# A graph network's dense output bank, its hot nodes' products and its counting one-hots, rearranged

## The chip, the cores and the metric

The kernel runs on one core of a Trainium2 chip. The metric is the device time of one execution in microseconds, the median over several runs. A profile comes from one more execution, recorded by the hardware profiler; its own time is given beside its span. Instructions run on TensorE (PE; its weight loads are PEld), VectorE (DVE), ScalarE (ACT), GpSimd (POOL) and SyncE (SP, which only issues DMAs). [...]

## The reference

There are 6250 nodes with 256 features, 100000 edges sorted by destination, and eight edge types. Three layers of a relational graph network run on x; the result is added to x and normalised. Then an attention layer and a second normalisation follow, which the change does not touch.

```python
for l in range(n_layers):                                   # 3
    xr = jnp.einsum('nd,rde->rne', x, W_rel[l])             # 8 matrices of 256 x 256
    msg = xr[edge_type, src]                                # one row per edge
    agg = jax.ops.segment_sum(msg, dst, num_segments=x.shape[0])
    x = jax.nn.relu(agg + x @ W_root[l] + bias[l])
```

The destinations are `6250 * u**2` for uniform `u`, sorted: low node numbers have very many edges. The first 4608 edges all end in about 16 nodes.

## The kernel before

**Order of operations.** The kernel sums source rows first and multiplies after: for each destination node and edge type it sums the source rows of x (the array S in SBUF, features on partitions), and a dense stage multiplies a node tile of 128 nodes by the eight relation matrices and the root matrix. Node tiles are called j, 49 of them; edges go in tiles t of 128, in groups of four.

**A step.** The loop of `layer` at L680 runs 193 steps in each of three layers, 188 of them with a group of edges. All instructions are written out by hand in this order (`manual_schedule`, L232), and each engine keeps it. A step does this:
- counting and hot products, if they are due (L681 to L684, below)
- `gather` (L474): four indirect DMAs on GpSimd bring the 4 x 128 source rows into a `msg` buffer, of which there are eight
- `onehot` (L458) on VectorE, for the group four steps later
- `finish` (L574) for a node tile whose dense products ended in the step before: bias on VectorE, relu on ScalarE, a store on SyncE; in the last layer also the sum with x and the normalisation. Then `clear` on ScalarE zeroes the tile's place in S
- `windows` (L483) on TensorE: rows times one-hot, into PSUM banks `pw`, of which there are four. A step uses one to four of them
- dense pieces (L704): up to six matmuls of the current tile, or more if several tiles are waiting; no further tile is begun in a step in which one ends
- `add` (L500) on VectorE: four additions of the windows into S. Each must wait for dense matmuls of a tile that is still being read from S, since the place in S is a register's value
- `turn` (L526): transposes of x rows for dense tiles that come up.

There are two interleaved streams of groups, each with its own ring in S (four and three node tiles long).

**The dense output.** `dense` (L553) takes a PSUM tile `pd` from the pool `ps_d`, which has one bank (L199). It issues two root products (L558) and sixteen relation products (L562). The bank is free again when `finish` has read it (L576, L579; L587 in the last layer).

**Hot nodes.** The edges of the first 36 edge tiles are not gathered. In layer 0, `count` (L609) makes a matrix A: how often each source node appears for each of the 16 hot nodes and each type. For a hot node n and each edge tile t that may hold edges of n, VectorE writes a one-hot `sel` of 392 columns (L622; three buffers) and, when t is new, a one-hot `low` (L618; 16 buffers); TensorE adds the product of both into a bank `ph` (L624); ScalarE copies the sum to A (L627). There are 138 pairs of n and t; steps from 56 on do two pairs each (COUNT_AT, L681), which ends at step 125. In every layer `products` (L630) multiplies A with all rows of x: 13 loads of four node tiles into a `msg` buffer through SyncE (L642, L640 for the partial last one), then the products (L651), all 49 into one bank `ph`. It moves on at every second step from 130 (HOT_AT, L683): the products of a load come two steps after the load, just before the next load. At the end ScalarE copies the sum (L653), TensorE transposes it (L657) and VectorE adds it to S (L660). The pool `ps_h` with one bank (L198) serves `count` and `products`.

**PSUM.** Eight banks: four `pw`, one `ph`, one `pd`, one for transposes (`pt`), one for a constant row (`iota`).

Of the kernel before, what the change touches and what calls it, by code (L numbers as in the profile page):

```python
# [10 lines left out]
F32 = mybir.dt.float32  # L11
I32 = mybir.dt.int32
BF16 = mybir.dt.bfloat16
AF = mybir.ActivationFunctionType
ALU = mybir.AluOpType
AX = mybir.AxisListType
PSUM = bass.MemoryType.PSUM
# [3 lines left out]
P = 128  # L21
# [3 lines left out]
PAD = 32  # L25
MARGIN = 800
HOT = 16
LOWS = 16
COUNT_AT = 56
HOT_AT = 130  # L30
NEAR = 450
# [123 lines left out]
def fast(tc, const, pl, x, xs, src, dst, edge_type, w_rel, w_root, bias, weight,  # L155
         attn_l, attn_r, out, flag):
    nc = tc.nc
    N, D = x.shape
    E = src.shape[0]
    L, R = w_rel.shape[0], w_rel.shape[1]  # L160
    H, DH = attn_l.shape
    KC = D // P
    NT, T, CH, WMAX = pl.NT, pl.T, pl.CH, pl.WMAX
    KR = KC * R

    with ExitStack() as top:
        tab = top.enter_context(tc.tile_pool(name="tab", bufs=1))
        ident = tab.tile([P, P], F32, name="ident")
        idx = tab.tile([P, CH * P], I32, name="idx")
        key = tab.tile([P, CH * P], F32, name="key")  # L170
        pos = tab.tile([1, CH * P], I32, name="pos")
        iota_p = tab.tile([P, 1], F32, name="iota_p")
        eps = tab.tile([P, 1], F32, name="eps")
        bias_b = tab.tile([P, L, D], F32, name="bias_b")
        w1x = tab.tile([P, KC, D + 2 * H], F32, name="w1x")
        altab = tab.tile([P, NT, H], F32, name="altab")

        psi = top.enter_context(tc.tile_pool(name="psi", bufs=1, space=PSUM))
        iota = psi.tile([P, max(R * WMAX, NT * R)], F32, name="iota")
        hk = tab.tile([P, pl.TH], F32, name="hk")  # L180
        hl = tab.tile([P, pl.TH], F32, name="hl")

        dram = top.enter_context(tc.tile_pool(name="lanes", bufs=1, space=DRAM))
        lane = dram.tile([NT * P], I32, name="lane")
        with tc.tile_pool(name="ps_p", bufs=2, space=PSUM) as ps_p:
            tables(tc, pl, ps_p, src, dst, edge_type, ident, idx, key, pos, iota, iota_p,
                   lane, hk, hl, flag, R, H)
        y = dram.tile([NT * P, D], F32, name="y")

        with ExitStack() as s:  # L190
            wp = s.enter_context(tc.tile_pool(name="wp", bufs=1))
            sp = s.enter_context(tc.tile_pool(name="sp", bufs=1))
            mp = s.enter_context(tc.tile_pool(name="mp", bufs=8))
            op = s.enter_context(tc.tile_pool(name="op", bufs=AHEAD + 2))
            xp = s.enter_context(tc.tile_pool(name="xp", bufs=3))
            hp = s.enter_context(tc.tile_pool(name="hp", bufs=1))
            ps_w = s.enter_context(tc.tile_pool(name="ps_w", bufs=4, space=PSUM))
            ps_h = s.enter_context(tc.tile_pool(name="ps_h", bufs=1, space=PSUM))  # L198
            ps_d = s.enter_context(tc.tile_pool(name="ps_d", bufs=1, space=PSUM))  # L199
            ps_t = s.enter_context(tc.tile_pool(name="ps_t", bufs=1, space=PSUM))  # L200


            S = [sp.tile([P, KR, n * P + PAD], F32, name=f"S{f}") for f, n in enumerate(NS)]

            hold = {j: sp.tile([P, KR, P], F32, name=f"hold{j}") for j in sorted(pl.shared(pl.TM))}


            A = hp.tile([P, NT, HOT * R], F32, name="A")

            nc.vector.memset(eps, EPS)  # L210
            for t in S:
                nc.scalar.memzero(t)
            nc.sync.dma_start(bias_b, bias.rearrange("l d -> (l d)").partition_broadcast(P))
            fold_weights(tc, mp, w1x, weight, attn_l, attn_r)

            def load_w(l):
                wr = wp.tile([P, KC, R, D], F32, name="wr")
                wo = wp.tile([P, KC, D], F32, name="wo")
                for k in range(KC):
                    nc.scalar.dma_start(  # L220
                        wr[:, k], w_rel[l, :, k * P:(k + 1) * P, :].rearrange("r p e -> p r e"))
                    nc.scalar.dma_start(wo[:, k], w_root[l, k * P:(k + 1) * P, :])
                return wr, wo

            groups = pl.order()

            ready = {}
            for i, (f, g) in enumerate(groups):
                for j in pl.reach(g):
                    ready[f, j] = i  # L230

            with tc.manual_schedule():  # L232
                for l in range(L):
                    wr, wo = load_w(l)
                    layer(tc, pl, l, l == L - 1, groups, ready, S, hold, A, hk, hl, idx, key, pos, iota, ident,
                          wr, wo, bias_b, x, xs, eps, w1x, altab, y,
                          mp, op, xp, hp, ps_w, ps_d, ps_t, ps_h, H)

        attention(tc, pl, lane, dst, idx, iota_p, ident, eps, w1x, altab, y, out, H)

# [199 lines left out]


def layer(tc, pl, l, final, groups, ready, S, hold, A, hk, hl, idx, key, pos, iota, ident, wr, wo,
          bias_b, x, xs, eps, w1x, altab, y, mp, op, xp, hp, ps_w, ps_d, ps_t, ps_h, H):
    nc = tc.nc
    N, D = x.shape
    KC = D // P
    R = wr.shape[2]
    NT = pl.NT
# [125 lines left out]
    def finish(j, pd):  # L574
        n = rows(j)
        nc.vector.tensor_tensor(pd[:, :D], pd[:, :D], bias_b[:, l], ALU.add)  # L576
        if not final:
            h = xp.tile([P, D], F32, name="h")
            nc.scalar.activation(h, pd[:, :D], AF.Relu)  # L579
            nc.sync.dma_start(xs[l + 1][j * P:j * P + n, :], h[:n])  # L580
            return
        xin = xp.tile([P, D], F32, name="xres")
        if n < P:
            nc.vector.memset(xin, 0.0)
        nc.sync.dma_start(xin[:n], x[j * P:j * P + n, :])
        z = xp.tile([P, D], F32, name="h")
        nc.vector.scalar_tensor_tensor(z, pd[:, :D], 0.0, xin, op0=ALU.max, op1=ALU.add)  # L587
        st = xp.tile([P, 6], F32, name="st")
        mv = xp.tile([P, 2], F32, name="mv")
        rs = xp.tile([P, 1], F32, name="rs")  # L590
        nc.vector.bn_stats(st, z)
        nc.vector.bn_aggr(mv, st)  # L592
        nc.scalar.activation(rs, mv[:, 1:2], AF.Sqrt, bias=eps)  # L593
        nc.vector.reciprocal(rs, rs)
        yt = xp.tile([P, D], F32, name="yt")
        nc.vector.tensor_scalar(yt, z, mv[:, 0:1], rs, op0=ALU.subtract, op1=ALU.mult)
        nc.sync.dma_start(y[j * P:(j + 1) * P, :], yt)
        return yt
# [9 lines left out]

    def count():  # L609

        lows = {}
        for n in range(HOT):
            tiles = pl.hot_tiles(n)
            pc = ps_h.tile([P, 512], F32, name="ph")
            for t in tiles:
                if t not in lows:
                    lows[t] = hp.tile([P, P], BF16, name="low", bufs=LOWS)
                    nc.vector.tensor_scalar(lows[t], iota[:, :P], hl[:, t:t + 1], None,  # L618
                                            op0=ALU.is_equal)
                    assert len([u for u in lows if u >= tiles[0]]) <= LOWS  # L620
                oh = hp.tile([P, NT * R], BF16, name="sel", bufs=3)
                nc.vector.tensor_scalar(oh, iota[:, :NT * R], float(512 * n), hk[:, t:t + 1],  # L622
                                        op0=ALU.add, op1=ALU.is_equal)
                nc.tensor.matmul(pc[:, :NT * R], lows[t], oh, start=(t == tiles[0]),  # L624
                                 stop=(t == tiles[-1]))
                yield
            nc.scalar.copy(A[:, :, n * R:(n + 1) * R],  # L627
                           pc[:, :NT * R].rearrange("p (j r) -> p j r", r=R))

    def products():  # L630

# [11 lines left out]
                    "(t p) d -> p t d", p=P))  # L643
            return t

        ph = ps_h.tile([P, 512], F32, name="ph")
        for js in loads:
            t = load(js)
            yield
            for n, j in enumerate(js):  # L650
                nc.tensor.matmul(ph[:, :D], A[:, j], t[:, n], start=(j == 0), stop=(j == NT - 1))  # L651
        sums = hp.tile([P, D], F32, name="sums")
        nc.scalar.copy(sums, ph[:, :D])  # L653
        yield
        pt = ps_t.tile([P, 4 * P], F32, name="pt")
        for k in range(KC):
            nc.tensor.transpose(pt[:, k * P:(k + 1) * P], sums[:, k * P:(k + 1) * P], ident)  # L657
# [22 lines left out]
    for i in range(NG + 5):  # L680
        for _ in range(2 if i >= COUNT_AT else 0):  # L681
            next(counting, None)
        if i >= HOT_AT and i % 2 == 0:  # L683
            next(hot, None)  # L684
        for j in sorted(fetch.get(i, []), reverse=True):
            held[j] = load_rows(j)
# [479 lines left out]
```

## Time and profile before

| | us |
|---|---|
| median of three runs | 3737.52 (3736.14 to 3748.91) |
| profiled execution | 3772.36 |
| its span | 3770.6 |
| TensorE busy | 2943.0 (78%) |
| TensorE weight loads | 2596.9 (69%) |
| GpSimd busy | 2155.9 (57%) |
| VectorE busy | 1740.8 (46%) |
| ScalarE busy | 481.0 (13%) |

The layers lie at about 60 to 1240, 1240 to 2405 and 2405 to 3600 us of the span, the attention behind them. Steps 56 to 126 of layer 0, with the counting, are 393.3 to 866.4 us; steps 130 to 158, with the hot products, follow in each layer.

A row of a group gives line, engine, operation, what is written and read, shape and number; then the busy time in us and the mean of one in ns; then the idle time of the engine just before these instructions and what ended most of it. In a timeline the columns are start and length in us, engine, line and operation, the number of instructions merged, and in brackets the idle time before and what ended it. "issue" stands where the profile names nothing that ended a wait, "remote" where it names no instruction. A matmul of f32 is recorded as two instructions. Ends of matmuls are modelled.

### The profile page before, as it was taken

The numbers are of one execution on the slowest core, as the hardware profiler recorded it, in microseconds if no ns is written. First come the engines' busy times: TensorE is split into PE (matmuls) and PEld (weight loads), VectorE is DVE, ScalarE is ACT, GpSimd is POOL, SyncE is SP. The second block draws the span as 40 slices with busy tenths as digits, with TensorE's granted clock in tenths as the row PEclk, the third lists the DMA queues.
The fourth block names the chain that finished last, engine by engine and source line by source line (L and its number), as shares of the span: only waits on it lengthen the run. The fifth ranks groups of instructions, "written<-read, shape, count | busy, mean of one in ns | idle before, by whom it ended". The sixth has DMA issues, their size and how long they took to land. (4 is left out here: it accounts for less than half of the span.)

```text
span 3770.6 us, 45208 instructions
## 1 busy us (share of the span) xinstructions
PE 2943.0 (78%) x15503; PEld 2596.9 (69%) x15504; DVE 1740.8 (46%) x4043; ACT 481.0 (13%) x646; POOL 2155.9 (57%) x2256
## 2 busy tenths in 40 slices
PE   3898878788777489888788866578988888877862
PEld 3787766677666378777677766567877777766752
DVE  5454555554333244444444323245555454433467
ACT  1111111110000011111111000011111110100033
POOL 5666555555664566666665666355666566566502
PEclk8999998889877699998988977789998898887786
DMA  4333222324432333333333433233333333443332
GB/s 124 103 105 101 87 87 88 90 85 123 134 96 73 106 100 105 101 104 102 100 97 115 138 103 99 86 90 102 104 110 101 101 108 98 124 128 103 89 121 94
DMA packets 201423, 389.11 MB, mean 103 GB/s; under 512 B 42661, under 2 KB 127652, under 8 KB 201188
## 3 DMA queue, kind: packets, MB, share of 16 engines
q0 software_dynamic: 107424, 293.48, 26.7%
q1 hardware_dynamic: 85832, 85.17, 7.1%
q10 hardware_dynamic: 7932, 7.48, 0.6%
q8 instruction: 129, 2.11, 0.2%
q14 instruction: 106, 0.87, 0.1%
HBM read 360.31 MB, written 25.65 MB: 102 GB/s over the span
## 5 line engine op out<-in xcount | busy, mean ns | idle before, releaser
L478 POOL DMA_INDIRECT msg<-x,idx x1492 | 1417.3, 950 | 954.7 <-issue 388.9
L495 PE MATMUL pw<-oh,msg 128*128 128x112 f32 (+6 forms) x8952 | 1461.7, 321 | 395.3 <-issue 188.5
L495 PEld LDWEIGHTS pw<-oh,msg 128*128 128x128 f32 x8952 | 1370.8, 213 | 504.8 <-issue 263.4
L507 DVE TENSOR_TENSOR S<-S,pw 128x224 f32 (+6 forms) x2238 | 954.3, 426 | 1598.6 <-remote 501.3
L562 PE MATMUL pd<-wr,S 128*128 128x256 f32 x4704 | 1180.9, 401 | 47.3 <-issue 31.5
L562 PEld LDWEIGHTS pd<-wr,S 128*128 128x128 f32 x4704 | 937.4, 203 | 198.9 <-issue 51.1
L478 POOL DMA_INDIRECT msg<-in_x_dram,idx x746 | 708.8, 950 | 487.1 <-issue 190.3
L462 DVE TENSOR_TENSOR oh<-iota,key 128x672 f32<-128x672 f32 (+8 forms) x564 | 388.6, 691 | 30.6 <-issue 16.9
L571 ACT ACTIVATE S<-S 128x2048 uint32<-128x2048 uint32 x150 | 285.0, 1900 | 0.1
L532 ACT COPY xT<-pt 128x256 f32<-128x256 f32 x196 | 72.8, 372 | 1254.5 <-PE pt L530 422.6
L558 PE MATMUL pd<-wo,xT 128*128 128x256 f32 x588 | 182.8, 439 | 45.7 <-ACT h L579 20.0
L579 ACT ACTIVATE h<-pd 128x256 f32<-128x256 f32 x98 | 37.7, 384 | 1172.3 <-DVE pd L576 753.7
L576 DVE TENSOR_TENSOR pd<-pd,bias_b 128x256 f32<-128x256 f32 x147 | 63.1, 429 | 219.6 <-PE pw L495 102.9
L558 PEld LDWEIGHTS pd<-wo,xT 128*128 128x128 f32 x588 | 116.4, 217 | 65.8 <-ACT h L579 24.8
L624 PE MATMUL ph<-sel,low 128*128 128x392 bf16 x138 | 43.3, 346 | 85.3 <-DVE sel L622 58.9
L847 POOL TENSOR_TENSOR pd<-yg,td 128x1792 f32<-128x1792 f32 x7 | 28.3, 4048 | 115.4 <-DVE td L845 48.9
L605 PE MATMUL pt<-w1x,xT 128*128 128x4 f32 x196 | 35.5, 287 | 66.4 <-ACT xT L532 44.3
L605 PEld LDWEIGHTS pt<-w1x,xT 128*128 128x128 f32 x196 | 31.2, 228 | 79.3 <-ACT xT L532 53.2
L622 DVE TENSOR_SCALAR sel<-iota,hk 128x392 bf16<-128x392 f32 x138 | 80.3, 613 | 0.0
L593 ACT ACTIVATE rs<-mv,eps 128x1 f32<-128x1 f32 x49 | 14.4, 295 | 482.5 <-DVE mv L592 338.9
L624 PEld LDWEIGHTS <-low 128*128 128x128 bf16 x138 | 13.2, 98 | 87.0 <-issue 48.5
L651 PE MATMUL ph<-msg,A 128*128 128x256 f32 x294 | 72.8, 391 | 0.0
(155 smaller groups left out, 749.7 us busy)
## 6 DMA issues: line engine op xcount, KB each, us to landing
msg<-x,idx POOLq DMA_INDIRECT x1492
x<-h SPq DMA_DIRECT2D x96, 128.0 KB
xin<-x SPq DMA_DIRECT2D x96, 128.0 KB
msg<-x SPq DMA_DIRECT2D x24, 512.0 KB
msg<-in_x_dram,idx POOLq DMA_INDIRECT x746
y<-yt SPq DMA_DIRECT2D x49, 128.0 KB
yg<-y SPq DMA_DIRECT2D x7, 896.0 KB
wr<-in_L_gnn_W_rel_dram ACTq DMA_DIRECT2D x6, 1024.0 KB
```

Of the source, the lines that this page charges most:

```text
L462: nc.vector.tensor_tensor(oh[:, :len(g), :w], iota[:, :w].unsqueeze(1).to_broadcast([P, len(g), w]), key[:, g[0]:g[-1] + 1].unsqueeze(2).t ...
L478: nc.gpsimd.indirect_dma_start(out=msg[:, q, :], out_offset=None, in_=table, in_offset=bass.IndirectOffsetOnAxis(ap=idx[:, t:t + 1], axis=0))
L495: nc.tensor.matmul(pw[:, k * w:(k + 1) * w], msg[:, q, k * P:(k + 1) * P], oh[:, q, :w], start=True, stop=True)
L507: ins = nc.vector.tensor_tensor(o, o, pw.rearrange("p (a b) -> p a b", b=W), ALU.add)
L532: nc.scalar.copy(xT.rearrange("p k n -> p (k n)"), pt[:, :D])
L558: nc.tensor.matmul(pd[:, :D], xT[:, k], wo[:, k], start=(k == 0), stop=False)
L562: i = nc.tensor.matmul(pd[:, :D], s[:, k * R + r], wr[:, k, r], start=False, stop=(k == KC - 1 and r == R - 1))
L571: i = nc.scalar.memzero(cols(f, j))
L576: nc.vector.tensor_tensor(pd[:, :D], pd[:, :D], bias_b[:, l], ALU.add)
L605: nc.tensor.matmul(pt[:, :H], yT[:, k], w1x[:, k, D + H:D + 2 * H], start=(k == 0), stop=(k == KC - 1))
L622: nc.vector.tensor_scalar(oh, iota[:, :NT * R], float(512 * n), hk[:, t:t + 1], op0=ALU.add, op1=ALU.is_equal)
L651: nc.tensor.matmul(ph[:, :D], A[:, j], t[:, n], start=(j == 0), stop=(j == NT - 1))
```

## The change

Three things change.

The pool `ps_h` goes, and `ps_d` has two banks. Dense tiles, the counts of a hot node and the hot products all take a bank from it, under the name `pd`.

In `count`, seven `sel` buffers (SELS) and eighteen `low` buffers (LOWS) let the one-hots of a pair be written five pairs (two and a half steps) before the pair's product. The bank is taken at a node's first product, and the copy to A stands right after its last.

In `products`, each load of four node tiles is summed in a bank of its own, and VectorE adds that bank to `sums` in SBUF (a copy for the first). The generator now moves on at every step: load at an even step, products at the odd step after it, addition at the next even step, before the next load. The final copy on ScalarE goes; the transposes follow the last addition in the same step.

Beside that the tiles `xres` and `yt` of the last layer have two buffers, not three.

```diff
-LOWS = 16
+SELS = 7
+LOWS = 18
...
-            ps_h = s.enter_context(tc.tile_pool(name="ps_h", bufs=1, space=PSUM))
-            ps_d = s.enter_context(tc.tile_pool(name="ps_d", bufs=1, space=PSUM))
+            ps_d = s.enter_context(tc.tile_pool(name="ps_d", bufs=2, space=PSUM))
...
-        xin = xp.tile([P, D], F32, name="xres")
+        xin = xp.tile([P, D], F32, name="xres", bufs=2)
...
-        yt = xp.tile([P, D], F32, name="yt")
+        yt = xp.tile([P, D], F32, name="yt", bufs=2)
...
-        lows = {}
-        for n in range(HOT):
-            tiles = pl.hot_tiles(n)
-            pc = ps_h.tile([P, 512], F32, name="ph")
-            for t in tiles:
+        lows, made, pc = {}, [], None
+        pairs = [(n, t) for n in range(HOT) for t in pl.hot_tiles(n)]
+        for m in range(len(pairs) + SELS - 2):
+            if m < len(pairs):
+                n, t = pairs[m]
                 if t not in lows:
                     lows[t] = hp.tile([P, P], BF16, name="low", bufs=LOWS)
                     nc.vector.tensor_scalar(lows[t], iota[:, :P], hl[:, t:t + 1], None,
                                             op0=ALU.is_equal)
...
-                oh = hp.tile([P, NT * R], BF16, name="sel", bufs=3)
+                oh = hp.tile([P, NT * R], BF16, name="sel", bufs=SELS)
                 nc.vector.tensor_scalar(oh, iota[:, :NT * R], float(512 * n), hk[:, t:t + 1],
                                         op0=ALU.add, op1=ALU.is_equal)
+                made.append((n, t, oh))
+
+            if m >= SELS - 2:
+                n, t, oh = made.pop(0)
+                tiles = pl.hot_tiles(n)
+                if t == tiles[0]:
+                    pc = ps_d.tile([P, 512], F32, name="pd")
                 nc.tensor.matmul(pc[:, :NT * R], lows[t], oh, start=(t == tiles[0]),
                                  stop=(t == tiles[-1]))
-                yield
-            nc.scalar.copy(A[:, :, n * R:(n + 1) * R],
-                           pc[:, :NT * R].rearrange("p (j r) -> p j r", r=R))
+                if t == tiles[-1]:
+                    nc.scalar.copy(A[:, :, n * R:(n + 1) * R],
+                                   pc[:, :NT * R].rearrange("p (j r) -> p j r", r=R))
+            yield
...
-        ph = ps_h.tile([P, 512], F32, name="ph")
+        sums = hp.tile([P, D], F32, name="sums")
         for js in loads:
             t = load(js)
             yield
+            ph = ps_d.tile([P, 512], F32, name="pd")
             for n, j in enumerate(js):
-                nc.tensor.matmul(ph[:, :D], A[:, j], t[:, n], start=(j == 0), stop=(j == NT - 1))
-        sums = hp.tile([P, D], F32, name="sums")
-        nc.scalar.copy(sums, ph[:, :D])
-        yield
+                nc.tensor.matmul(ph[:, :D], A[:, j], t[:, n], start=(n == 0), stop=(j == js[-1]))
+            yield
+            if js[0] == 0:
+                nc.vector.tensor_copy(sums, ph[:, :D])
+            else:
+                nc.vector.tensor_tensor(sums, sums, ph[:, :D], ALU.add)
...
-        if i >= HOT_AT and i % 2 == 0:
+        if i >= HOT_AT:
             next(hot, None)
```

## Prediction

> **What bounds the kernel now.** First the page: the profiled execution took 3772.4 us, its span 3770.6, 34.8 us over the median of the runs (3737.5); I take differences from it in us and subtract them from the median. TensorE is busy 2943.0 us (78%), GpSimd 57%, VectorE 46%. By stages, TensorE is 85 to 91% busy in 300 us early in each layer (100 to 400, 1400 to 1700, 2500 to 2800) and the clock's mean is 0.876. Next the timeline: the gather of a step is issued 35 to 50 us before the windows that use it, seven steps ahead, and its last packet lands 2.4 us after the issue. So the gathers wait for buffers that TensorE frees, and TensorE with the waits in its own queue sets the time. The chain of waits holds only the last 5 us and tells nothing here.
>
> Then the windows view over the same steps (56 to 126) of the three layers; columns are the stretch, its length, busy us of PE, PEld, DVE, ACT, POOL, granted clock, DMA share, GB/s:
>
> ```profile
> 393.30:866.40 473.10, 385.22 (x2001) 335.31 (x2001) 260.30 (x552) 55.20 (x72) 257.67 (x272) 0.89 0.29 86
> 1615.30:2026.10 410.80, 344.85 (x1865) 307.33 (x1866) 181.49 (x382) 47.98 (x57) 258.64 (x273) 0.92 0.34 100
> 2795.60:3222.30 426.70, 363.17 (x1985) 326.02 (x1986) 216.30 (x500) 53.62 (x77) 260.00 (x274) 0.90 0.35 102
> ```
>
> Only layer 0 counts, and takes 62.3 us more than layer 1 for it: 40.4 of TensorE work, 21.9 of idleness. The waits of TensorE there (total, times, longest):
>
> ```profile
> PE ph L624 <- DVE sel L622: 55.9, 48, 4.5
> PE ph L624 <- issue: 17.5, 15, 4.0
> PE ph L624 <- DVE low L618: 6.1, 2, 3.3
> ```
>
> They are nearly all of its 87.9 idle us. The timeline of one step shows why:
>
> ```profile
> 828.00 1.89 PE L562 MATMUL pd<-wr,S 128*128 128x256 f32 x8
> 829.51 0.10 PEld L624 LDWEIGHTS <-low 128*128 128x128 bf16 x1
> 829.93 2.12 DVE L507 TENSOR_TENSOR S<-S,pw 128x336 f32 x4 [3.37 <-PE pd L562]
> 831.97 1.15 DVE L622 TENSOR_SCALAR sel<-iota,hk 128x392 bf16<-128x392 f32 x2
> 832.64 0.33 PE L624 MATMUL ph<-sel,low 128*128 128x392 bf16 x1 [2.75 <-issue]
> 833.54 0.33 PE L624 MATMUL ph<-sel,low 128*128 128x392 bf16 x1 [0.57 <-ACT A L627]
> ```
>
> VectorE may add to S only after the dense matmuls have read it, the one-hots stand behind those adds, the count's matmul behind the one-hot, and all windows behind it. Last, what the first dense matmul of a tile waits for, in the whole kernel:
>
> ```profile
> L558 PE MATMUL pd<-wo,xT 128*128 128x256 f32 x588 | 182.8, 439 | 45.7 <-ACT h L579 20.0 <-issue 12.9 <-DVE h L587 12.6
> ```
>
> I worked out from the loop in which step each tile starts and is evacuated, and set the gaps at L558 beside it: every one of over 0.3 us but one (0.7 us, step 182 of layer 0) lies in a step in which a tile starts while the one before it is evacuated; there are 26 such steps a layer. There the tile's bank is free only when bias (VectorE) and relu (ScalarE) are through with it; in the last layer the reader is the sum with x, L587.
>
> [...] The trace has half and full speed only; fewer gaps may add speed, which I don't count. [...]
>
> **One-hots ahead (count).** Removed from TensorE's path: its gaps before L624, 71.0 us before the first product of a step and 14.3 before the second, 85.3. No instruction is removed: 138 one-hots (617 ns) and 36 lows (339 ns) stay, two and a half steps ahead of their products; LOWS grows since a low lives that much longer; the stage ends two steps later (127), before the hot loads at 130. Three things come back. First, relu waits: the count holds one of the two banks, so dense has one, as before. In ten steps a tile starts while the last is evacuated. After the dense end VectorE does adds 2.1, two one-hots 1.2, next step's one-hot 0.85, bias 0.43, then relu 0.38 and handovers: about 5.0 us. TensorE without the stall does products 0.4 and windows 2.4 and is there after some 3.2: 1.8 us in ten steps, 18. Second, the copy of a count (0.49 us plus handovers, 0.7) stands between two nodes in the same step, eight times if the same bank is taken: 5. Third, window banks: the first add frees one 0.5 us after the dense end; the products fill that time. Nothing; if they don't, 70 x 0.2 = 14. That would leave 62. But layer 1 counts nothing and still idles 65.9 us here, in stretches where adds wait for TensorE up to 11 us. Layer 1 plus products (69 pairs x 0.4, by 0.49 for a pair and 0.1 hidden, = 28) plus 18 - 6.8 = 11 more of relu waits (6.8 are in layer 1's time) is 449.8: gain 23. I take 33, nearer to the second, as those stretches may also come here. Bounds 12 and 65.
>
> **Second bank for dense.** Removed: the 45.7 us at L558 less what stays: 4.0 in layer 0's count stage, where the count holds the other bank, 0.2 in the hot stage, where a part holds it, and the 0.7 of step 182. That is 40.8: 9.9 in layer 0, 18.2 in layer 1, 12.6 in layer 2. Elsewhere the two banks alternate, and a tile is evacuated two or more steps before its bank returns. Bias and relu themselves stay (429 and 384 ns) but hide behind the new tile's first products. What comes next is the add after the dense part, which moves forward by the same amount, and with it the windows' banks; so nearly all counts: 34. Bounds 0 (rival 2) and 41.
>
> **Hot products in parts.** Added: 13 instructions a layer on VectorE, 39 x 424 ns (the row of L587, a read of the same width[...]) = 16.5 us; three ScalarE copies (373 ns) go. VectorE is 36 to 39% busy in the three hot stages; if nothing hid them, 16.5. A part is a bank's sum over four node tiles, added to sums in SBUF. Products use the loaded rows one step after the load, not two. Each load stays at its even step and its SyncE place behind the last stores. From issue to the next step's windows there are at least 9.3 us for the full loads, and a pair of loads lands 3 to 8 us after its first issue (about 4.5 to 7 for most): no wait, at worst 2 us in four. The last, partial load has 5.8, 5.2 and 3.6 us and lands after 4.8 to 5.9: 3 us in all. At the end the transposes now wait for the last part's add behind the step's adds, 2.5 us x 3 = 7.5; in return the old transposes' waits, 17.6 us, go in part: say 8. The rows' buffers come free a step sooner, worth nothing as gathers are three steps ahead there. Sum: a loss of 3; bounds a loss of 20 and a gain of 8. Deeper xres and yt buffers are given up at no cost: finishes two apart are five steps or more apart, a yt is read after two. If that cover failed, one VectorE wait of some 3 us for each of 49 tiles, 147.
>
> **Sum.** 33 + 34 - 3 = 64 us, 1.7%: 3772.4 becomes 3708, the median 3737.5 becomes 3673.5. A measurement of this kernel tells about 0.5% (18.7 us) from no change.
>
> **Rivals.** (1) The count's stall moves: what TensorE no longer waits for at L624 it waits for at windows and relu, gain 10 instead of 33: 3696.5. For it: layer 1's idleness. Against: in the step shown nothing else was late. (2) The pool gives the next tile the bank just freed, so the second bank does nothing: 3737.5 - (33 - 3) = 3707.5. Against: eight msg buffers are used in turn, seven steps deep. (3) More gain: 62 for the count, 41 for dense, 3 lost, and a little clock: 3635. For it: the idle sums; against: layer 1. (4) Slower: the hot loads come late. One step of lead is lost for each of 39 loads; if SyncE, behind stores that wait for relu (104.7 us of waits in layer 0's hot stage), issues them so late that each product waits 3 us, that is 117, and 3673.5 + 117 = 3790 follows. It makes the kernel slower by over 0.5% above (64 + 18.7)/39 = 2.1 us a load. Leads of 9 us against 7 of landing speak against it.
>
> **Chances.** Likeliest case (gain 40 to 85) 0.60; rival 1 0.14; rival 2 0.09; rival 3 0.09; rival 4 0.05; nothing gained for reasons not seen 0.03. Below 3718.8 lie the likeliest, rival 3 and most of 1 and 2: faster 0.84; same 0.10; slower 0.06. Range 3642 to 3714: the likeliest case alone is 3652 to 3697; the range goes on to rivals 1 and 2 and leaves out rivals 3 and 4 and what is unseen, 0.17.
>
> **What would show it.** Right: the gaps before the count's matmul (now from ph to pd) fall from 85 to under 15 us, that stage from 473 to about 440; L558 idle falls to about 10, what is left lying in steps 56 to 126. Wrong: L558 gaps unchanged; L651 with gaps at all (now 0.4 us in sum); new gaps at L495 after DVE adds; layers 1 and 2 not shorter by 10 to 18 us each. What would break the whole sum is layer 1's idleness: if it belongs to a busy TensorE, what is taken off one wait returns in another.

## The result, and the profile after

Over eight runs each, the kernel before takes 3738.38 us (3722.18 to 3759.57), the changed one 3696.16 us (3683.15 to 3716.37). The ratio is 0.9883, with a 95% interval of 0.9847 to 0.9919: 42 us faster, where 64 was forecast. The profiled execution of after took 3689.81 us, its span 3688.0, its granted clock 0.877 (0.876 before). It was 6 us below the median of its kernel; that of before, 3772.36, was 34 above its own and above all eight of its runs. So the two spans differ by 82.6 us and the medians by 42: about 40 us of what the pair of profiles shows is the spread between executions, and a stage's difference from it can carry any part of that.

First the page of after, part 1: busy us, share of the span and instructions of each engine.

```profile
PE 2921.8 (79%) x15503; PEld 2587.1 (70%) x15504; DVE 1746.9 (47%) x4082; ACT 477.8 (13%) x643; POOL 2148.1 (58%) x2256
```

TensorE is busy 21 us less than before with the same number of instructions, so three quarters of the 82.6 are idle time. The windows view of after over steps 56 to 126 of the three layers (stretch, length, busy us of PE, PEld, DVE, ACT, POOL, clock, DMA share, GB/s):

```profile
386.30:813.50 427.20, 369.92 (x2002) 320.76 (x2003) 259.90 (x559) 54.31 (x71) 259.00 (x274) 0.91 0.33 96
1557.70:1966.30 408.60, 347.17 (x1864) 308.79 (x1865) 181.43 (x383) 47.80 (x56) 260.00 (x275) 0.91 0.35 101
2725.80:3142.80 417.00, 359.10 (x1984) 322.79 (x1985) 216.06 (x500) 53.53 (x77) 259.15 (x274) 0.92 0.36 105
```

The counting stage is 46 us shorter, the same steps of layers 1 and 2 only 2 and 10. Of the 46, 15 is TensorE work. Measured from the windows of one step to those of another, the other stretches differ so: steps 0 to 56 of the three layers by -5.8, -5.9 and -6.3 us, the steps with hot products (126 to 158) by +1.4, -2.7 and -8.5, the steps behind them by -0.4, -1.0 and +5.5.

What TensorE waits for in the counting stage of after (total, times, longest):

```profile
PE pd L558 <- ACT h L579: 11.6, 5, 3.2
PE pd L632 <- ACT A L635: 8.5, 5, 3.9
PE pw L495 <- DVE S L507: 6.4, 11, 1.7
PE pd L632 <- issue: 5.9, 3, 2.8
...
PE pd L558 <- ACT A L635: 3.4, 1, 3.4
```

The one-hots are gone from the list. The two waits that the prediction put in their place are there: for relu and for the copy of a count. And the groups of after, for the whole kernel:

```profile
L495 PE MATMUL pw<-oh,msg 128*128 128x112 f32 (+6 forms) x8952 | 1446.7, 319 | 422.1 <-DVE S L507 175.5 <-issue 159.0 <-remote 37.8
L558 PE MATMUL pd<-wo,xT 128*128 128x256 f32 x588 | 186.2, 444 | 20.4 <-ACT h L579 11.6 <-issue 5.1 <-ACT A L635 3.4
L661 PE MATMUL pd<-msg,A 128*128 128x256 f32 x294 | 73.8, 395 | 1.9 <-DMA msg<-in_x_dram 1.9
L632 PE MATMUL pd<-sel,low 128*128 128x392 bf16 x138 | 37.4, 344 | 15.3 <-ACT A L635 8.5 <-issue 5.9 <-ACT h L579 0.9
```

The idle time ahead of the count's matmul fell from 85.3 to 15.3, ahead of the first dense matmul of a tile from 45.7 to 20.4, and 17.1 of the 20.4 lie in steps 56 to 128 of layer 0. The loads of the hot rows are late by 1.9 us in all. But the windows' idle time, the first row, grew: before, it was this.

```profile
L495 PE MATMUL pw<-oh,msg 128*128 128x112 f32 (+6 forms) x8952 | 1461.7, 321 | 395.3 <-issue 188.5 <-DVE S L507 109.3 <-remote 44.8
```

The windows wait 26.8 us longer, 66 longer behind VectorE's adds. That is close to the 25.3 us that left the dense matmuls' wait, but they do not lie in the same stages. In the counting stage the windows' idle time rose by 17.2 us (1.6 to 18.8), and L558's rose too (4.0 to 17.1). Outside of it L558 lost 38.4 us, the windows gained 9.6, and all of TensorE's idle time fell by 30.8. In this pair the next wait took up only a part. How much of it is the spread between executions, one pair cannot tell.

### The profile page after: what moved, and what is told of

Read it like the earlier page. It is cut to its first block, busy times and chain, and to the rows that moved or that the text cites. A ratio compares the mean times of both kernels' runs of the same rounds, so it can differ in the third digit from the quotient of the medians.

```text
span 3688.0 us, 45176 instructions
## 1 busy us (share of the span) xinstructions
PE 2921.8 (79%) x15503; PEld 2587.1 (70%) x15504; DVE 1746.9 (47%) x4082; ACT 477.8 (13%) x643; POOL 2148.1 (58%) x2256
## 5 line engine op out<-in xcount | busy, mean ns | idle before, releaser
L495 PE MATMUL pw<-oh,msg 128*128 128x112 f32 (+6 forms) x8952 | 1446.7, 319 | 422.1 <-DVE S L507 175.5
L495 PEld LDWEIGHTS pw<-oh,msg 128*128 128x128 f32 x8952 | 1356.8, 211 | 526.8 <-issue 226.4
L562 PE MATMUL pd<-wr,S 128*128 128x256 f32 x4704 | 1187.7, 402 | 56.2 <-issue 40.8
L562 PEld LDWEIGHTS pd<-wr,S 128*128 128x128 f32 x4704 | 940.5, 204 | 211.4 <-issue 61.7
L558 PE MATMUL pd<-wo,xT 128*128 128x256 f32 x588 | 186.2, 444 | 20.4 <-ACT h L579 11.6
L558 PEld LDWEIGHTS pd<-wo,xT 128*128 128x128 f32 x588 | 120.6, 223 | 36.9 <-ACT h L579 12.6
L661 PE MATMUL pd<-msg,A 128*128 128x256 f32 x294 | 73.8, 395 | 1.9 <-DMA msg<-in_x_dram 1.9
L530 PE MATMUL pt<-ident,xin 128*128 128x128 f32 x294 | 59.2, 284 | 14.5 <-issue 8.2
L661 PEld LDWEIGHTS pd<-msg,A 128*128 128x128 f32 x294 | 57.1, 201 | 9.9 <-issue 2.6
```

Source lines behind the costliest of these rows:

```text
L495: nc.tensor.matmul(pw[:, k * w:(k + 1) * w], msg[:, q, k * P:(k + 1) * P], oh[:, q, :w], start=True, stop=True)
L558: nc.tensor.matmul(pd[:, :D], xT[:, k], wo[:, k], start=(k == 0), stop=False)
L562: i = nc.tensor.matmul(pd[:, :D], s[:, k * R + r], wr[:, k, r], start=False, stop=(k == KC - 1 and r == R - 1))
L661: nc.tensor.matmul(ph[:, :D], A[:, j], t[:, n], start=(n == 0), stop=(j == js[-1]))
```

## The experiments

The expectations put three accounts, called theories, against each other. In A all parts add up, each at about half of what the two traces show, so that the one-hots and the second dense bank give about half of the gain each. In B the stages of the traces have their true sizes. In C the count's part is all. Most experiments undo one part or do one part alone. The smaller `xres` and `yt` go with the new `count` and with the second bank; they were not tried apart, but `bank_only` has them and loses nothing.

One thing must be known of all of them. They ran on three chips, on which the kernel before takes 3163.55, 3167.25 and 3162.58 us, 15% less than in the result. No chip is on record for the result; that it was another one is inferred from the times. Each kernel is compared with before on its own chip. So they settle which part works there and by which mechanism; sizes hold for those chips. Here is the page of before there, part 1 and two groups:

```profile
PE 2733.6 (87%) x15503; PEld 2465.2 (78%) x15504; DVE 1742.1 (55%) x4043; ACT 480.5 (15%) x646; POOL 2152.6 (68%) x2256
...
L478 POOL DMA_INDIRECT msg<-x,idx x1492 | 1415.4, 949 | 516.0 <-issue 405.1 <-PE pw L495 40.2 <-DMA wr<-in_L_gnn_W_rel_dram 40.0
...
L558 PE MATMUL pd<-wo,xT 128*128 128x256 f32 x588 | 167.7, 411 | 0.0
```

TensorE is idle 425 us (3158.9 less 2733.6) and not 828. A gather takes GpSimd as long as on the other chip (949 ns here, 950 there), but TensorE needs 209 us less for the same instructions, at a clock of 0.932. The third row already speaks against half of the prediction: the dense matmuls wait for no bank at all here.

### Before, once more

No edit; it shows how far two sets of runs of one kernel differ. It was also to tell which stages of the profiled execution of before had been slow; from another chip it can't.

> The kernel before against itself: ratio 1 within the interval. Its profile tells how much stages vary from one execution to the next: if the profiled execution of before was a slow one (theory A), this one is nearer to the median, some 35 us shorter, and the shortening is spread over stages; if steps 56 to 126 of layer 0 alone stay at 473 us while the others shrink, the count's part keeps its size of about 40 us and another part must be smaller.

3162.7 us, ratio 1.0 (0.9992 to 1.0008).

### The whole change

No edit; after, on one of these chips.

> The whole change once more. If it runs on a chip like that of the first four runs, where GpSimd issues a gather every 1.25 us without waiting outside the counting steps, the second bank and the parts have nothing to give there and the whole is what the one-hots ahead give: 95 to 105 us faster than before, and steps 56 to 126 of layer 0 take about 353 us, which is 70 steps of four gathers at 1.26 us. If it runs on a chip where TensorE sets the time, as in the result, 40 to 80 us faster.

3063.81 us, ratio 0.9675 (0.9662 to 0.9688): 103 us faster, more than twice the 42 of the result.

### One-hots ahead alone

The kernel before with the new `count` in its own bank:

```diff
-                oh = hp.tile([P, NT * R], BF16, name="sel", bufs=3)
+                oh = hp.tile([P, NT * R], BF16, name="sel", bufs=SELS)
...
+                made.append((n, t, oh))
...
+            if m >= SELS - 2:
+                n, t, oh = made.pop(0)
+                tiles = pl.hot_tiles(n)
+                if t == tiles[0]:
+                    pc = ps_h.tile([P, 512], F32, name="ph")
```

> One-hots for the counts five pairs ahead, alone: count and hot products keep their own bank, dense its one bank. Theory A (the three parts add up, each about half of what the two traces show, as the profiled execution of before was a slow one): 20 to 30 us faster than before, steps 56 to 126 of layer 0 fall from 473 to 435 us or less, layers 1 and 2 stay as before. Theory B (the traces' stages are the true sizes, 46 for the count): 46 us faster. Theory C (the count's part is all there is): 42 us faster and the second bank alone gives nothing. The gaps at L558 in the count stage rise from 4 to about 17 us, since dense has one bank there in either kernel.

3065.36 us, ratio 0.9685 (0.9672 to 0.9698): 98 us. That is nearly all of the whole change's 103, and three times the 33 of the prediction. The waits at L558, expected at about 17 us in the count stage, are 4.8 in the whole kernel. This part holds earlier one-hots, a bank taken later and a copy right after the last product; these were not tried apart.

### The second bank alone

The kernel before with `count` and `products` as they were, in the shared pool:

```diff
-            ps_h = s.enter_context(tc.tile_pool(name="ps_h", bufs=1, space=PSUM))
-            ps_d = s.enter_context(tc.tile_pool(name="ps_d", bufs=1, space=PSUM))
+            ps_d = s.enter_context(tc.tile_pool(name="ps_d", bufs=2, space=PSUM))
```

> The second bank alone: two banks shared by dense, count and hot products, but each one-hot still just ahead of its product, and the hot products in one sum that holds a bank from step 132 to 156. Theory A: 12 to 20 us faster. Theory B: 30 us faster. Theory C: no change. In all three the gaps at L558 outside steps 56 to 126 of layer 0 and the hot steps fall from 41 us to under 3, and the first 56 steps of layers 1 and 2 become 6 us shorter each.

3162.9 us, ratio 0.9995 (0.9987 to 1.0003): nothing, within 0.1%.

### Hot products in parts alone

The kernel before with the new `products`, in the count's old bank, at every step:

```diff
+            ph = ps_h.tile([P, 512], F32, name="ph")
...
-                nc.tensor.matmul(ph[:, :D], A[:, j], t[:, n], start=(j == 0), stop=(j == NT - 1))
+                nc.tensor.matmul(ph[:, :D], A[:, j], t[:, n], start=(n == 0), stop=(j == js[-1]))
...
+                nc.vector.tensor_tensor(sums, sums, ph[:, :D], ALU.add)
...
-        if i >= HOT_AT and i % 2 == 0:
+        if i >= HOT_AT:
```

> The hot products in parts of four node tiles alone, with their own bank, loads at even and products at odd steps; everything else as before. Theory A: within 8 us of before. Theory B: 10 us faster in the steps 126 to 158. If the products' lost step of lead mattered, 39 loads would each be waited for by some 2 us, 78 us slower; the gaps before the products then show a DMA as what ended them. The transposes at the end wait for the last addition by some 12 us a layer, as in the changed kernel, where they waited for ScalarE by 6 before.

3159.5 us, ratio 0.9984 (0.9976 to 0.9991): 4 to 5 us faster, where a loss of 3 was forecast. The steps with the products are 10.0 us longer in the three layers together (2.5, 6.0 and 1.5) and those behind them 14.9 shorter (2.8, 6.2 and 5.9). The transposes wait 7.0 us in the three layers, where 12 a layer were expected.

### After without the one-hots ahead

After with the old `count`, taking its bank from the shared pool (`sel` with three buffers, one-hot and product in the same step).

```diff
-                oh = hp.tile([P, NT * R], BF16, name="sel", bufs=SELS)
+                oh = hp.tile([P, NT * R], BF16, name="sel", bufs=3)
```

> The change without its one-hots ahead: two shared banks, hot products in parts. On a chip where GpSimd sets the pace outside the count: within 8 us of before, and steps 56 to 126 of layer 0 stay at their old length. On a chip where TensorE sets it: 15 to 40 us faster (the second bank and parts).

3160.32 us, ratio 0.9978 (0.9969 to 0.9987): 7 us are left of 103. They agree with what the parts give alone, and leave a second bank nothing beyond 2 or 3 us.

### After with one dense bank

One bank for dense, one for the counts and the parts.

```diff
-            ps_d = s.enter_context(tc.tile_pool(name="ps_d", bufs=2, space=PSUM))
+            ps_h = s.enter_context(tc.tile_pool(name="ps_h", bufs=1, space=PSUM))
+            ps_d = s.enter_context(tc.tile_pool(name="ps_d", bufs=1, space=PSUM))
...
-                    pc = ps_d.tile([P, 512], F32, name="pd")
+                    pc = ps_h.tile([P, 512], F32, name="ph")
```

> The change without its second bank for dense: one bank for dense, one for count and parts, one-hots ahead. Where GpSimd sets the pace: equal to the whole change within 4 us, since the gaps of TensorE at L558 are then covered by its waiting for gathers. Where TensorE sets it: the 41 us of gaps at L558 come back, the time is 20 to 35 us over that of the whole change, and the first 56 steps of layers 1 and 2 are 6 us longer each.

3064.49 us, ratio 0.9675 (0.9662 to 0.9688): the same as after. The bank is worth nothing here once the one-hots are out of the way, either. The first dense matmuls now wait 5.0 us (3.2 in after), and the time does not change.

### After without the parts

The products are summed in one bank of the shared pool again, at every second step.

```diff
-                nc.tensor.matmul(ph[:, :D], A[:, j], t[:, n], start=(n == 0), stop=(j == js[-1]))
+                nc.tensor.matmul(ph[:, :D], A[:, j], t[:, n], start=(j == 0), stop=(j == NT - 1))
...
-        if i >= HOT_AT:
+        if i >= HOT_AT and i % 2 == 0:
```

> The change without the parts: one-hots ahead, two shared banks, but all hot products in one sum that holds a bank for 26 steps, two steps after each load. Where GpSimd sets the pace: 0 to 8 us over the whole change (parts alone gave 4). Where TensorE sets it: within 10 us of it, either way.

3068.58 us, ratio 0.9692 (0.9678 to 0.9705), 5 us over after: the parts gain the same 5 whether added to before or taken from after.

### What the count's part is made of

The windows view over steps 56 to 126 of layers 0 and 1, of before on these chips:

```profile
318.50:765.30 446.80, 377.93 (x2001) 332.03 (x2001) 260.92 (x552) 54.98 (x72) 263.42 (x279) 0.90 0.33 94
1363.10:1701.60 338.50, 318.29 (x1864) 291.77 (x1865) 183.64 (x385) 47.74 (x56) 256.25 (x271) 0.96 0.42 120
```

and of after there:

```profile
315.10:664.90 349.80, 335.79 (x2001) 298.19 (x2002) 259.15 (x560) 54.48 (x73) 262.97 (x278) 0.99 0.41 118
1267.20:1603.60 336.40, 314.66 (x1865) 288.84 (x1866) 183.57 (x385) 47.65 (x56) 254.77 (x269) 0.98 0.41 120
```

The counting stage alone is 97 us shorter, in two halves. TensorE's idle time falls from 68.9 to 14.0 us, 55. And its busy time falls from 377.9 to 335.8, 42 us, at the same 2001 instructions, while the granted clock of the stage rises from 0.90 to 0.99. Layer 1, in whose same steps nothing of the order changed, keeps length and busy time within 4 us. In the trace the clock goes to half in 18 stretches of at most 6.8 us in the stage of before, and in one stretch in that of after. What TensorE waited for in that stage before:

```profile
PE ph L624 <- DVE sel L622: 65.1, 55, 3.3
PE ph L624 <- ACT A L627: 3.0, 5, 0.7
PE pw L495 <- DVE S L507: 0.6, 1, 0.6
```

and after:

```profile
PE pw L495 <- DVE S L507: 6.1, 13, 1.7
PE pd L632 <- ACT A L635: 4.2, 7, 0.7
PE pd L558 <- ACT h L579: 3.2, 1, 3.2
```

65.1 us of waits for one-hots, in 55 gaps of 3.3 at most, are replaced by 14 in short ones, none of them for a gather. TensorE is then busy for 96% of the stage. GpSimd's own waits in it, before:

```profile
POOL msg L478 <- PE pw L495: 100.9, 41, 5.5
POOL msg L478 <- issue: 71.2, 233, 0.6
```

and after:

```profile
POOL msg L478 <- issue: 76.8, 252, 0.3
POOL msg L478 <- PE pw L495: 7.9, 18, 1.1
```

Before, the gathers waited 100.9 us for buffers that TensorE had to free; after, they are issued nearly back to back. 70 steps of four gathers at 0.95 us and 0.30 of issue each are 350 us, and the stage is 349.8 long. This does not make GpSimd the bound of the stage: the gathers of a step are issued 18 to 36 us ahead of its windows all through it, and 23 us more of GpSimd's work lengthen it by only 4.8 (below). The 349.8 are TensorE's 335.8 and its 14.0 of waits; that the two sums agree is chance.

### TensorE made busier

If a bank is worth nothing because GpSimd sets the pace, it should be worth something when TensorE does. In three kernels the windows of two of the four edge tiles of a group are multiplied twice (the second time into the same place, with the same values).

```diff
-                nc.tensor.matmul(pw[:, k * w:(k + 1) * w], msg[:, q, k * P:(k + 1) * P],
-                                 oh[:, q, :w], start=True, stop=True)
+                for _ in range(2 if n < 2 else 1):
+                    nc.tensor.matmul(pw[:, k * w:(k + 1) * w], msg[:, q, k * P:(k + 1) * P],
+                                     oh[:, q, :w], start=True, stop=True)
```

In before:

> The kernel before with more work on TensorE: the windows of two of a step's four edge tiles are multiplied twice into the same place, 8 more recorded matmuls a step, some 1.1 us, so that TensorE and not GpSimd should set the pace; nothing else is changed and the values are the same. 188 x 3 steps of 5.0 us become about 6: 450 to 650 us slower than before. If waits for the dense bank are a matter of a busy TensorE, the gaps at L558, none before on this chip, come back with 30 to 50 us.

3549.56 us, 387 over before, where 450 to 650 were expected. The waits at L558 that were to come back are nil. In after:

> The changed kernel with the same extra work on TensorE. If the result's 42 us (against 103 on this chip) come from TensorE setting the pace in all steps there, the change is worth 40 to 90 us against the kernel before with the same extra work, and the gaps at L558 lie in steps 56 to 126 of layer 0 alone. If not, it stays at about 100 and the second bank still gives nothing.

3440.35 us, 109 less. In after with one dense bank:

> The change without its second bank for dense, with the same extra work on TensorE. If the second bank is worth what the gaps say once TensorE sets the pace, this is 20 to 40 us slower than the changed kernel with the extra work, with 30 to 40 us of gaps at L558. If the wait is only moved to the next one, within 8 us of it.

3438.46 us: still nothing for the bank. Ratios to before without the double windows are 1.1228 (1.1209 to 1.1247), 1.0877 (1.0859 to 1.0895) and 1.0878 (1.086 to 1.0896). TensorE did become the bound (93% busy in `pe_after`, where GpSimd waited 409 us for buffers), and even then no first dense matmul waits over 0.3 us for its bank in any of the three. The test has a weak point: the added windows stand between the end of a tile and the first matmul of the next, and so leave bias and relu more time. Two stages without added work have no such flaw. In steps 0 to 56 of layer 0 and 56 to 126 of layer 2 TensorE waits for no gather in before on these chips either, and the second bank alone takes 284.1 and 349.0 us there, against 284.2 and 347.6. So the idea that only GpSimd's pace hid the bank's worth falls. In `pe_after` (lines shifted by one) the hot nodes' transposes wait as follows, 7.0 us where the prediction had 7.5:

```profile
PE pt L670 <- DVE sums L667: 7.0, 3, 2.3
```

### GpSimd made busier

After, with one write of 128 x 256 by GpSimd in each step:

```diff
+            spare = hp.tile([P, 256], F32, name="spare")
+            nc.gpsimd.memset(spare, 0.0)
```

> The changed kernel with one zeroing of 128 x 256 on GpSimd added in each of the 564 steps with gathers. If GpSimd's issue of gathers sets the pace outside the count, nearly each of these counts, with 0.3 us of issue: 564 x (its recorded length + 0.3), some 250 to 350 us slower than the changed kernel, and 70 steps of the count become as much longer as others. If TensorE sets it, under 30 us.

3149.65 us, ratio 0.9962 (0.9948 to 0.9977): about 86 over after. The group of the added instruction:

```profile
L702 POOL MEMSET spare<- 128x256 f32 x564 | 186.2, 330 | 0.2
```

It fills 186.2 us, of which 86 count; 250 to 350 were expected, with an issue time of 0.3 that did not come. By stages, steps 56 to 126 of layer 0 are 4.8 us longer, of layer 1 21.3 and of layer 2 0.0, for 23 us of added work in each. So GpSimd's time sets the pace in some stages after the change, and not in the counting stage.

## Why the prediction was right or wrong

**Direction and range: right.** 3696.16 lies in the range, and on every chip the change is faster. The sum, 64 for 42, holds two errors that partly cancel: too little for the count and, on the experiments' chips, too much for the bank. That the time lies in the range is in part luck.

**"One-hots ahead (count)": mechanism right, size too small.** That the stall goes and nothing of its size takes its place is shown: alone it gives 98 us of 103 on the experiments' chips, and without it 7 us are left. On the result's chip the counting stage is 46 us shorter in one pair of profiles. The step that mis-sized it is the comparison with layer 1, which led from 62 to 33: it took the idleness of a stage that the change doesn't touch for a floor of the stage that it does. By it the stage would have kept 77 us of idle time (449.8 less 344.85 and 28); it kept 57.3 on the result's chip and 14.0 on the others. Its ground was misread, too: in the waits of VectorE in layer 1 the gaps of 11 us and more stand as "remote" and "issue", and those for TensorE's dense matmuls end at 7.8. The returning waits were 18 for relu and 5 for the copy; in the result's pair L558's waits in this stage were 17.1 and those behind the copy 8.5, so these terms were near. The third term, window banks, had an estimate of nothing, 14 at worst: 6.4 stand there behind VectorE's adds, and the windows' idle time in the stage rose by 17.2 in all.

**"fewer gaps may add speed, which I don't count": wrong to leave out.** On the experiments' chips the clock in the stage rose from 0.90 to 0.99, and the same 2001 instructions took 42 us less, more than two fifths of the part's gain. With 65.1 us of gaps for one-hots, of 3.3 us at most, the trace has 18 stretches at half clock in the stage; without them, one. So less idleness goes with a higher clock here; which gaps lower it was not tried. On the result's chip the stage's clock rose only from 0.89 to 0.91 (20 stretches at half before, 12 after, none over 6.8 us), with 15 us less busy time.

**"Second bank for dense": 34 forecast, nothing found on the experiments' chips.** The bank alone, the change without it, and both under a busier TensorE give zero within 3 us. In the trace, the gaps that were to be removed (45.7 us) do not exist on those chips: 0.0. What fails there is the step before "nearly all counts": it took the gaps at L558 for a property of the kernel's order, whereas with the same order they come and go with the chip. Take those of the prediction's 26 steps a layer that lie in layers 0 and 1 and outside of the count: the bias starts 1.7 us after the recorded end of the last dense matmul on the result's chip and 0.04 us after it in before on a faster one (medians). Relu is done after 2.7 and 0.96 us. On the faster chip the windows last until 1.97 us, and so cover it. The last section shows why the bias is late.

For the result's chip the bank's share stays open. The stages that only the bank could have shortened there (steps 0 to 56 of each layer, 56 to 126 of layers 1 and 2) shrank by about 30 us in a pair of profiles whose executions lie 40 us apart for no reason of the change, and 46 for the count alone already fills the 42 of the medians. If the 40 us were spread evenly over the two executions, which no run tests, some 41 would be left for the count and 9 for these stages; that is an estimate from their lengths. So rival 2, in which the bank does nothing, is right in its outcome on the experiments' chips; its reason, that the pool hands out the bank just freed, is not what happened, as L558's gaps outside of the count fell from 41.7 to 3.3 us on the result's chip.

**"Hot products in parts": -3 forecast, +5 measured**, inside its bounds. The loads were late by 1.9 us in the result's profile, not 3 in all or 3 each, so rival 4 falls. On the experiments' chips the transposes at the end wait 7.0 us; before they waited 2.8. On the result's chip they waited 17.6 and now wait 36.7, as this row of its whole-kernel waits has it:

```profile
PE pt L669 <- DVE sums L666: 36.7, 3, 14.1
```

The estimate of 7.5 assumed VectorE's adds on time; there they were not (last section). Why the steps behind the products become shorter by more than the products cost was not tried, nor were the transposes one step later.

**"TensorE with the waits in its own queue sets the time".** It holds on the result's chip, where GpSimd is seven steps ahead of the windows. On the others it holds in the counting stage, before the change and after it, which is why the gain there ends at 97: TensorE has 14.0 us of idle time left. In other stages GpSimd's 1.25 us a gather takes part in setting the pace: TensorE waits 116.5 us for gathers in after there, all outside of the count.

**What was to show it.** The gaps ahead of the count's matmul were to fall under 15 us (15.3), the stage to about 440 (427.2), L558's idle time to about 10 (20.4), layers 1 and 2 to be 10 to 18 us shorter each (11.7 and 18.9, from the stretches above up to step 187). Most came near; L558 could not fall to 10, as the prediction itself had 18 us of relu waits return there. Two signs of being wrong came as well: the windows' waits behind VectorE's adds grew by 66 us, and the hot products had a gap of 1.9 us, for a load. And the bank's share was wrong where it could be tried: signs from one pair of executions bear out an account without telling it from its rivals.

**The other rivals.** Rival 1 named 3696.5, the measured time to within 0.4 us, for the wrong reason: it had the count's stall move to windows and relu and leave 10 us. In the counting stage of the result's chip 17 us did move to the windows and 13 to relu, of 85, and the count's part gave nearly everything where it was tried. Rival 3 had the count at 62, nearest to its 46 to 98, but with 41 for the bank beside it.

**The base.** Subtracting a gain from the median was sound. Comparing stages in one execution 34 us over that median was not good to better than such an amount, and the prediction gave no width for it.

## What to carry to other kernels

A wait of the busiest engine behind another engine's queue can be worth more than its own length: here 65.1 us of waits gave 97, with the clock at 0.99 instead of 0.90 once they were gone. So move the producer ahead of the work that it queues behind, and count the clock. A gap that the wait view puts on a buffer need not be worth its length (on the result's chip 25.3 us less of gaps at L558 came with 26.8 more ahead of the windows); take the buffer away and measure before giving it a price. An engine whose work adds up to the length of a stage (GpSimd's 350 us in 349.8) need not be its bound: see whether another one waits for it. A single profiled execution can differ from its kernel's median by as much as a small change is worth (34 us here, for a change of 42), so check it against the median first.

## What the runs showed of the hardware

The same kernel took 3738 us in the result and 3163 to 3167 on three other chips. Of the 611 us between the two spans of before (3770.6 and 3158.9), 209 are TensorE's busy time and 402 its idle time.

On the slower chip VectorE often starts well after the last recorded matmul that it needs. Its adds have, in after there, this row of waits, "remote" being one that the profile gives no instruction for:

```profile
DVE S L507 <- remote: 584.9, 149, 19.9
```

On the faster chips the same view has no such row; in before there it names TensorE's matmuls of L495 and L562 for 941.2 of the 1053.2 us that VectorE is idle before these adds. The traces also hold the instants at which TensorE's completions are counted on a semaphore; in before on the slower chip 1356 of the 2238 adds are recorded as waiting on it. In before on a faster chip practically all of 2211 are there within 0.1 us of the recorded end of their matmul. On the slower chip 47% are, and about 750 come over 1 us late; the shares are rough, since 1934 are recorded. Here is step 39 of layer 1 in before, on the slower chip:

```profile
1509.79 2.87 PE L495 MATMUL pw<-oh,msg 128*128 128x200 f32 x16
1512.50 2.75 PE L562 MATMUL pd<-wr,S 128*128 128x256 f32 x12
1515.43 2.59 DVE L507 TENSOR_TENSOR S<-S,pw 128x400 f32 x4 [5.17 <-PE pd L562]
...
1520.70 1.49 PE L558 MATMUL pd<-wo,xT 128*128 128x256 f32 x4 [2.60 <-ACT h L579]
```

and on a faster one:

```profile
1275.88 2.87 PE L495 MATMUL pw<-oh,msg 128*128 128x200 f32 x16
1276.76 2.60 DVE L507 TENSOR_TENSOR S<-S,pw 128x400 f32 x4 [0.41 <-PE pw L495]
1278.59 2.75 PE L562 MATMUL pd<-wr,S 128*128 128x256 f32 x12
...
1282.95 1.04 PE L558 MATMUL pd<-wo,xT 128*128 128x256 f32 x4
```

The kernel is the same, and so are the lengths of the windows and dense matmuls. The windows of the four edge tiles end 0.84 to 2.87 us after the first one starts. On the faster chip their completions come at 0.85 to 2.88 us. On the slower one the first four that are recorded come together, at 5.62 to 5.79 us, and the first add starts 20 ns after the first of them. The view puts the wait down to the dense matmuls, as the last of them had ended just before. Bias and relu stand behind these adds, at 1519.81 and 1520.26 us on the slower chip, and the next tile's first matmul behind relu, at 1520.70. So the gap at L558 arises here on this chip and not on the other, and by the medians given with the second bank most others do likewise.

A longer case is step 155 of layer 0 in after, where no completion of TensorE's is recorded between 991.91 and 1002.45 us:

```profile
1002.48 1.92 DVE L507 TENSOR_TENSOR S<-S,pw 128x288 f32 x4 [18.58 <-remote]
...
1004.78 0.69 PE L669 MATMUL pt<-ident,sums 128*128 128x128 f32 x2 [11.32 <-DVE sums L666]
```

The dense matmuls are recorded as ended at 993.47; the adds begin 9 us later, and TensorE waits 11.32 us for an add behind them. Why completions come late on this chip stays open, as no experiment ran on it.
